# Values of two batches' contexts made in the router's tail and passed through device memory to the last attention of a two-layer decoder

## The chip, the cores and the metric

The kernel runs on one core of a Trainium2 chip. The metric is the device time of one execution in microseconds (us), the median of several runs. A run with a profile gives in addition a record of every instruction on the engines: PE (matmuls; PEld is its weight loads), DVE (vector), ACT (scalar), POOL (GpSimd), and SP, which here only issues DMA transfers. Each engine takes its instructions in one order that is fixed when the program is built, and waits on semaphores for what other engines and transfers have to finish.

## The reference

A decoder of two layers works on x (4 batches, 512 tokens, 256 features, float32) with a context of 1601 tokens of 256 features for each batch. After each step the sum with x is normalised. The steps are:

1. layer 0: a sequential fast-weight recurrence over the tokens;
2. layer 0: cross attention with one head on the context, with an additive mask;
3. layer 0: a mixture of 8 experts, of which a router picks 2 for each token;
4. layer 1: causal self attention with 16 heads of 16 features;
5. layer 1: cross attention on the same context with 16 heads and rotary positions;
6. layer 1: a feed-forward block with quantised weights.

The parts that the change touches, cut from the reference:

```python
# step 3, for each token
probs = softmax(xf @ Wr + br)
topw, topi = top_k(probs, 2)
# step 5
K = (key @ Wk.T + bk)        # key and value are the context, (4, 1601, 256)
V = (value @ Wv.T + bv)      # split into 16 heads of 16
out = softmax(rope(Q) @ rope(K).T / 4) @ V
x = layernorm(x + out @ Wo.T + bo)
```

The bias `bv` is folded into the bias after the output product, so the kernel's values are the plain product of the context with `Wv`. They depend on inputs alone and could be made at any time.

## The kernel before

Everything is float32. Tokens lie in tiles of 128 partitions: a batch's x is 4 such tiles (`x[b]`), its transpose is `xT[b]`, and a context is 13 key tiles, the last with 65 rows. The program is a sequence of stages. Within most of them the order of the instructions on every engine is the order of the Python program (`manual_schedule`), written out by hand; between them a scheduler may interleave.

**Step 2 and the router.** The loop over 16 steps (batch, token tile) computes scores with `ctxT`, exponents, transposed weights and the weighted context. When a batch is through, a generator `closing(b)` is put into the list `tails`; each call of `tail()` runs it to its next `yield`. It normalises the batch (`rstd_ln`: two ACT instructions), transposes it into `xT[b]` (eight PE transposes and one ACT copy, lines 188 and 196), and runs `route(b)`: four groups of products with `Wr` (8 columns wide), an exp on ACT (line 470), a chain of small DVE instructions that pick two experts, two products that count rows before (`before`, `full`), and DVE instructions that make `rows`. `scatter(b)` (line 534) then writes the batch's rows to their experts' places in `xs` in device memory, by eight indirect DMAs that POOL issues. The scatters of batches 0 to 2 are ordered among each other: each waits until the one before has landed. Those of batch 3 are declared free of order. For batches 0 to 2 the generator's pieces lie between other batches' steps. For batch 3 nothing is left to lie between: the last loop, `while tails: tail()`, runs it alone. PSUM tiles called `bank` come from a pool of two, tiles called `wide` from a pool of three.

**The experts.** `begin(i)` loads the 256 rows of block i (`xb`, line 835) and its weights `eWi` and `eWg`; `first_half` loads `eWo`. Blocks follow one another on PE with 48 matmuls of 256 columns each (two records in the trace for each matmul). Eight weights of layer 1 (`W`, 256 KB each) are loaded on SP before the first block; their tiles lie where the tiles of step 2 lay, and wait for those.

**Layer 1.** There are 32 units (batch, group of four heads, self or cross), first the 16 of the self attention, then the 16 of the cross attention, batch by batch. In a cross unit a loop runs over 13 key tiles. Each step computes four score tiles (line 1315), their exponents on ACT (line 1329), the weighted values of the tile before (`po`, line 1342), and two slots of the next unit's row maxima (PE line 202, `one<-kc,qt`, and DVE line 1272). Work of other kinds is spread over the steps from the list `extras[i]` of unit i, one item behind a step. Where a step has an item, `po` is computed 512 columns wide in one piece; where it has none, in two pieces of 256, each in one half of the step (`filled`).

Items of the list are, among others, the keys and values of later batches, made by `context(b, keys, values)`: a key item is two matmuls of 512 columns with a part of the context (`cx`, loaded by `chunk`), an ACT copy with bias and a rotation on POOL, after which the rows go through device memory (`kcd`); a value item is two matmuls of 256 columns with `W["xaV"]` and an ACT copy (line 1196) that puts 16 heads of 16 columns at a distance of 17 into `vals[b % 2]`. The free 17th column holds 1.0 and the last 15 columns 0.0, set once by `values_tile`. Values and keys of batches 0 and 1 are made earlier, around the start of layer 1. For batches 2 and 3 the list `later` deals them out: to the four cross units of batch 0 the keys of batch 2 and half of those of batch 3, to those of batch 1 the other half and the 13 value items of batch 2, to those of batch 2 the 13 value items of batch 3. Work that has to run at the start of a unit lies in `starts[i]`; the loads of `kc` are there.

Of the kernel before, what the change touches and what calls it, by code (L numbers as in the profile page):

```python
# [9 lines left out]
F32 = mybir.dt.float32  # L10
# [7 lines left out]
P = 128  # L18
B, S, D = 4, 512, 256
S2 = 1601  # L20
NT = S // P
NKT = (S2 + P - 1) // P
# [3 lines left out]
NH, HD = 16, 16  # L26
# [8 lines left out]
def kn_of(kt):  # L35
    return P if kt < NKT - 1 else KLAST
# [3 lines left out]
def decoder(ctx: ExitStack, tc: tile.TileContext, a: dict, out: bass.AP):  # L40
    nc = tc.nc
# [13 lines left out]
    def wide():  # L55
        return psum["A"].tile([P, 2, 512], F32, tag="wide", name="wide")

    def bank():
        return psum["B"].tile([P, 512], F32, tag="bank", name="bank")
# [15 lines left out]
    def weight(pool, name):  # L75

        src = a[name]
        t = pool.tile([P, 2, src.shape[1]], F32, tag=name, name=name)
        nc.sync.dma_start(t, src.rearrange("(c p) n -> p c n", p=P))
        return t  # L80
# [117 lines left out]
    def mm(ps, terms):  # L198

        n = len(terms)  # L200
        for i, (l, r) in enumerate(terms):
            nc.tensor.matmul(ps, l, r, start=(i == 0), stop=(i == n - 1))  # L202
# [3 lines left out]
    p2in = ph2in.enter_context(tc.tile_pool(name="p2in", bufs=1))  # L206


    with (
# [15 lines left out]
        ps = wide()  # L225
# [4 lines left out]
        ps = bank()  # L230
# [7 lines left out]
        fs = p2in.tile([P, NT, S2], F32, tag="fs", name="fs")  # L238
# [7 lines left out]
        KHALF = (NKT + 1) // 2  # L246
# [281 lines left out]
    def scatter(b, done=lambda inst: None):  # L528

        rows = placed[b]  # L530
        for t in range(NT):
            for k in range(2):
                done(
                    nc.gpsimd.indirect_dma_start(
                        xs, bass.IndirectOffsetOnAxis(ap=rows[:, k * NT + t : k * NT + t + 1], axis=0), x[b][:, t, :], None
                    )
                )
# [67 lines left out]
        return wrow, xrow  # L605


    with tc.tile_pool(name="p2", bufs=2) as p2, ExitStack() as ordered:


# [5 lines left out]
        ps = wide()  # L616
# [3 lines left out]
        ps = bank()  # L620
# [3 lines left out]
        ps = wide()  # L624
# [3 lines left out]
        ps = bank()  # L628
# [25 lines left out]
        def scored(b, t):  # L654

            blk = slice(t * P, (t + 1) * P)
            sc = p2.tile([P, S2], F32, tag="sc", name="sc")
            mx = small.tile([P, 2], F32, tag="mx", name="mx")
            for h, (k0, kw) in enumerate(parts):
                ps = wide()  # L660
                flat = ps.rearrange("p a n -> p (a n)")
                for s0 in range(0, kw, 512):
                    s1 = min(s0 + 512, kw)
                    mm(
                        flat[:, s0:s1],
                        [(qs[b][:, c, blk], ctxTs[b][:, c, k0 + s0 : k0 + s1]) for c in range(2)],
                    )
                nc.vector.tensor_tensor_reduce(
                    out=sc[:, k0 : k0 + kw],
                    in0=flat[:, :kw],  # L670
                    in1=fs[:, t, k0 : k0 + kw],
                    scale=1.0,
                    scalar=LOWEST,
                    op0=ALU.add,
                    op1=ALU.max,
                    accum_out=mx[:, h : h + 1],
                )
            nm = small.tile([P, 1], F32, tag="nm", name="nm")
            nc.vector.tensor_reduce(nm, mx, AX.X, ALU.max, negate=True)
            sm = small.tile([P, 1], F32, tag="sm", name="sm")  # L680
            nc.scalar.activation(sc, sc, AF.Exp, bias=nm, accum_out=sm)
            scs[b, t], sums[b, t] = sc, sm
# [59 lines left out]
        scored(*steps[0])  # L742
        tails = []

        def tail():
            if tails and next(tails[0], tails) is tails:
                tails.pop(0)

        for i in range(len(steps) + 1):
            if i + 1 < len(steps):  # L750
                b, t = steps[i + 1]
                scored(b, t)
                if t == NT - 1:
                    more_columns(b + 2)
                    if b + 1 < B:
                        queries(b + 1)
            tail()
            if i < len(steps):
                turned(*steps[i])
            tail()  # L760
            if i > 0:
                b, t = steps[i - 1]
                weighted(b, t)
                if t == NT - 1:
                    if b + 1 < B:
                        ctxns[b + 1] = load_ctx(b + 1)
                    tails.append(closing(b))
            tail()
        while tails:
            tail()  # L770
        ordered.close()
        scatter(B - 1, lambda inst: unordered("xs", inst))
        wrow, xrow = blocks_left()
# [5 lines left out]


    QS = 1.0 / math.sqrt(HD)
    VW = HD + 1
    p4a = late_a.enter_context(tc.tile_pool(name="p4a", bufs=1))
    mrow = tc.dram_tile((4 * B, S2), F32, name="mrow")
    live = p4a.tile([P, 4 * B], F32, tag="live", name="live")
# [27 lines left out]
    def values_tile(pool, name, n):  # L813
        t = pool.tile([P, n, NH * VW + HD - 1], F32, tag=name, name=name)
        nc.gpsimd.memset(t[:, :, NH * VW :], 0.0)
        heads = t[:, :, : NH * VW].rearrange("p k (h r) -> p k h r", r=VW)
        nc.gpsimd.memset(heads[:, :, :, HD : HD + 1], 1.0)
# [210 lines left out]
    with ExitStack() as s4:  # L1028
# [149 lines left out]
        def context(b, keys, values, here=None):  # L1178


            def key(src, i, c, eng):
                flush(1)
                k0, kw = chunks[i]
                ps = one()
                mm(ps[:, :kw], [(W["xaK"][:, h, c * P : (c + 1) * P], src()[h][:, :kw]) for h in range(2)])
                raw = raw_tile()
                nc.scalar.activation(raw[:, :kw], ps[:, :kw], AF.Identity, bias=bkc[:, c : c + 1])
                rotated(raw, kw, slice(k0, k0 + kw), eng, ready["turn", i] if here else None)
                going.append(lambda: to_rows(kcd[b], c, k0, kw, raw[:, :kw]))

            def value(src, k):
                kn, c0 = kn_of(k), (k % 4) * P
                ps = one()[:, :D]
                mm(ps[:kn], [(src()[c][:, c0 : c0 + kn], W["xaV"][:, c, :]) for c in range(2)])
                dst = vals[b % 2][:kn, k, : NH * VW].rearrange("p (h r) -> p h r", r=VW)
                nc.scalar.copy(dst[:, :, :HD], ps[:kn].rearrange("p (h r) -> p h r", r=HD))

            items = []
            for i in sorted({*keys, *values}):
                if here is None:  # L1200
                    src = lambda n=len(stream): chunk(n)
                    stream.append((b, i))
                else:
                    src = lambda i=i: here[2 * i : 2 * i + 2]
                eng = nc.gpsimd if here is None else nc.vector
                if i in keys:
                    items += [lambda s=src, i=i, c=c: key(s, i, c, eng) for c in range(2)]
                if i in values:
                    items += [lambda s=src, k=k: value(s, k) for k in range(4 * i, min(4 * i + 4, NKT))]
            return items  # L1210
# [121 lines left out]
        def weighted(u, k, q0=0, q1=S):  # L1332
# [6 lines left out]
            for j in range(4):  # L1339
                ex = state["ex", u, k, j // 2]  # L1340
                c0 = (4 * g + j) * VW
                nc.tensor.matmul(  # L1342
# [227 lines left out]
        for b in range(1, B):  # L1570
            i = index[b - 1, 0, False]
# [11 lines left out]
        for b in range(B):  # L1583
            i = index[b - 1, 0, True] if b else index[B - 1, 0, False]
# [30 lines left out]
        flush(0)  # L1615
        for i, (n0, n1) in enumerate(((0, 4), (4, 6), (6, 7), (7, 8))):
            extras[i] = keys1[n0:n1] + extras[i]
        later = [
            context(2, range(4), ()) + context(3, range(2), ()),
            context(3, range(2, 4), ()) + context(2, (), range(4)),  # L1620
            context(3, (), range(4)),
        ]
        for b, work in enumerate(later):
            for g in range(NG):
                n = -(-len(work) // (NG - g))
# [5 lines left out]
        for b in range(B - 1):  # L1631
            i = index[b, NG - 1, True] + 2
# [10 lines left out]
        for i, u in enumerate(units):  # L1643
# [16 lines left out]
            for k in range(nk):  # L1660
# [13 lines left out]
                for half in range(2 if u != units[-1] else 0):  # L1674
                    first = scores(u, k, half, 0)
# [33 lines left out]
        rest = ending()  # L1709
# [149 lines left out]
```

## Time and profile before

| | |
|---|---|
| median of 3 runs | 2454.46 us (2454.04 to 2455.28) |
| the profiled execution | 2460.01 us, its span 2458.2 us |
| mean granted PE clock | 0.964 |
| busy: PE, DVE, ACT, POOL | 2349.0, 1187.0, 1074.2, 425.0 us |
| last products of step 2 to the first expert's transposes | 485.4 to 521.4 us |
| experts | 521.4 to about 1020 us |
| cross attention of layer 1 | about 1510 to 2334 us |

The page's second part divides the span into 40 equal slices of 61.5 us and gives the busy share of an engine in each as one digit, 9 for 90% or more. The timeline gives the start and the length in us, the engine, the line, the operation, `out<-in` by the names of the tiles, shapes, and how many instructions were merged (`x8`); in brackets stands how long the engine had been idle before and what ended that. `SPq` and `POOL ... DMA_INDIRECT` are the issues of transfers, not their landing. A stage table gives the busy time of each engine in a stretch, then the granted clock (1.00 is full), the DMA share and GB/s. A PE instruction's own length overlaps the next one's, so a chain is read from start to start.

### The profile page before, as it was taken

What the parts mean: (1) busy time and instruction counts of PE and PEld (TensorE: products, weight loads), DVE (VectorE), ACT (ScalarE), POOL (GpSimd) and SP (SyncE); (2) the same over time, 40 slices, a digit from 0 to 9 for tenths busy, and PEclk for the clock granted to TensorE, in tenths of its full rate; (3) what the DMA queues carried; (4) which work ended last, traced back from release to release, by engine and by line L of the source; (5) the groups of instructions that cost most, each with busy time, mean ns of one, the idle gap of its engine ahead of it and who ended that gap; (6) DMA issues with size and microseconds to landing.
All of it is one profiled execution on the core that took longest, in us unless ns stands there. A gap on an engine that the chain in (4) does not pass through costs nothing.

```text
span 2458.2 us, 34942 instructions
## 1 busy us (share of the span) xinstructions
PE 2349.0 (96%) x13928; PEld 1331.3 (54%) x13928; DVE 1187.0 (48%) x2772; ACT 1074.2 (44%) x1996; POOL 425.0 (17%) x431
## 2 busy tenths in 40 slices
PE   7998999959999999969999999999999999999998
PEld 4767677748888888743333334333333333333256
DVE  1333334422222222336666667666666666677334
ACT  1111222114455544324555553655566565556730
POOL 1010001121134444323330000222110010000000
PEclk9999999969999999978999998999999999999999
DMA  8300211234767555442211220122210110110100
GB/s 319 135 1 23 102 54 44 73 135 149 263 251 273 212 190 197 145 122 81 83 44 30 71 75 5 49 73 62 66 54 20 44 40 16 32 36 16 33 9 26
DMA packets 82513, 224.50 MB, mean 91 GB/s; under 512 B 14120, under 2 KB 37934, under 8 KB 73262
## 3 DMA queue, kind: packets, MB, share of 16 engines
q1 hardware_dynamic: 68190, 141.70, 17.1%
q0 software_dynamic: 10992, 65.54, 7.3%
q10 hardware_dynamic: 3168, 15.03, 1.8%
q8 instruction: 110, 1.80, 0.3%
q14 instruction: 53, 0.43, 0.1%
HBM read 171.53 MB, written 53.21 MB: 91 GB/s over the span
## 4 chain that ended last, share of the span: by engine, by line
PE 51%; ACT 1%; DVE 1%; issue 0%; DVEq 0%; ACTq 0%
PE s L1315 23%; PE one L202 12%; PE po L1342 11%; PE s L202 2%; PE s L1325 1%; PE one L1300 1%; PE one L1363 1%; ACT x L171 0%; ACT ex L1329 0%; DVE one L1274 0%; PE one L1384 0%; PE one L1405 0%; PE one L1482 0%; DVE pm L1272 0%; DVE st L156 0%
## 5 line engine op out<-in xcount | busy, mean ns | idle before, releaser
L1329 ACT ACTIVATE ex<-s 128x512 f32<-128x512 f32 (+1 forms) x1062 | 578.1, 594 | 480.5 <-PE s L1315 237.4
L1272 DVE TENSOR_REDUCE pm<-one 128x1 f32<-128x512 f32 x768 | 494.2, 686 | 203.7 <-PE s L1315 147.7
L1315 PE MATMUL s<-q,kc 32*128 32x512 f32 x1612 | 522.9, 640 | 0.2 <-ACT ex L1329 0.2
L202 PE MATMUL one<-kc,qt 32*128 32x512 f32 (+1 forms) x2048 | 483.6, 563 | 0.3 <-DVE pm L1272 0.3
L1315 PEld LDWEIGHTS s<-q,kc 32*128 32x128 f32 x1612 | 161.6, 179 | 210.2 <-issue 175.2
L1342 PE MATMUL po<-ex,v 128*32 128x256 f32 (+3 forms) x2472 | 245.8, 466 | 0.3 <-ACT ot L1355 0.3
L1274 DVE CUSTOM_DVE_ANT_0 one<-one,c_diagq 128x512 f32<-128x512 f32 x256 | 172.0, 716 | 89.2 <-PE one L202 78.3
L1315 PE MATMUL s<-q,ks 32*128 32x512 f32 x512 | 182.2, 660 | 4.9 <-ACT ex L1329 4.9
L1342 PEld LDWEIGHTS po<-ex,v 128*32 128x32 f32 (+1 forms) x2472 | 49.9, 108 | 233.0 <-issue 227.0
L886 DVE TENSOR_TENSOR g<-g,sg 128x1024 f32<-128x1024 f32 x46 | 57.3, 1246 | 238.3 <-ACT sg L883 238.3
L202 PE MATMUL wide<-xbT,eWi 128*128 128x256 f32 x736 | 168.4, 388 | 4.0 <-DVE xbT L858 4.0
L202 PEld LDWEIGHTS one<-kc,qt 32*128 32x128 f32 x2048 | 163.9, 188 | 11.7 <-DVE pm L1272 7.7
L202 PE MATMUL bank<-eWo,g 128*128 128x256 f32 x736 | 162.8, 379 | 0.5 <-DVE rb L899 0.5
L202 PE MATMUL wide<-xbT,eWg 128*128 128x256 f32 x736 | 162.9, 379 | 0.1
L202 PEld LDWEIGHTS wide<-xbT,eWi 128*128 128x128 f32 x736 | 143.6, 195 | 25.1 <-issue 3.4
L1155 POOL TENSOR_TENSOR raw<-raw,c_cos 128x512 f32<-128x512 f32 (+1 forms) x32 | 35.0, 1093 | 696.2 <-DMA swp<-raw 616.5
L202 PE MATMUL one<-ks,qt 32*128 32x512 f32 x512 | 153.4, 668 | 1.1 <-ACT raw L1126 1.1
L202 PEld LDWEIGHTS wide<-xbT,eWg 128*128 128x128 f32 x736 | 139.8, 190 | 19.5 <-ACT g L883 0.5
L202 PEld LDWEIGHTS bank<-eWo,g 128*128 128x128 f32 x736 | 138.1, 190 | 18.5 <-DVE rb L899 0.6
L883 ACT ACTIVATE g<-wide,eWi 128x256 f32<-128x256 f32 x184 | 71.9, 477 | 69.8 <-PE wide L202 67.0
L1315 PEld LDWEIGHTS s<-q,ks 32*128 32x128 f32 x512 | 54.1, 188 | 83.1 <-issue 61.9
L202 PE MATMUL wide<-ctxT,q 128*128 128x512 f32 (+1 forms) x256 | 91.3, 510 | 0.8 <-DVE q L649 0.8
(310 smaller groups left out, 2969.7 us busy)
## 6 DMA issues: line engine op xcount, KB each, us to landing
xs<-zero SPq DMA_DIRECT2D x32, 512.0 KB
kc<-kcd SPq DMA_DIRECT2D x16, 800.5 KB
eWo<-in_eWo SPq DMA_DIRECT2D x8, 1408.0 KB
cx<-in_ctxT SPq DMA_DIRECT2D x18, 512.0 KB
eWi<-in_eWi SPq DMA_DIRECT2D x8, 1028.0 KB
eWg<-in_eWg SPq DMA_DIRECT2D x8, 1028.0 KB
swp<-raw SPq DMA_DIRECT2D x64, 128.0 KB
qt<-qd SPq DMA_DIRECT2D x32, 256.0 KB
```

What stands on the lines that cost most here:

```text
L202: nc.tensor.matmul(ps, l, r, start=(i == 0), stop=(i == n - 1))
L883: nc.scalar.activation(dst[:, k, :], pv[:, k, :], func, bias=bias)
L886: nc.vector.tensor_tensor(part, part, dst, ALU.mult)
L1155: eng.tensor_tensor(raw[:, :n], raw[:, :n], cos[:, :n], ALU.mult)
L1272: nc.vector.tensor_reduce(pm[:, t, j, c : c + 1], ps, AX.X, ALU.max)
L1274: nc.vector.tensor_tensor_reduce(out=ps, in0=ps, in1=diagq[:, 384 - t * P : 896 - t * P], scale=1.0, scalar=LOWEST, op0=ALU.add, op1=ALU.m ...
L1300: nc.tensor.transpose(pt[:, t * P : (t + 1) * P], ng.rearrange("p j r -> p (j r)"), ident)
L1315: nc.tensor.matmul(ps[:kn], kt[rows, k * P : k * P + kn], q2[rows, :], start=True, stop=cross)
L1325: nc.tensor.matmul(ps[:, k * P : (k + 1) * P], later_[:, :P], later_[:, P:], start=False, stop=True)
L1329: nc.scalar.activation(ex[:kn, h, :], ps[:kn], AF.Exp)
L1342: nc.tensor.matmul(state["po"][j * 32 : j * 32 + 32, q0:q1], (vals if cross else vself)[b % 2][:kn, k, c0 : c0 + 32], ex[:kn, j % 2, q0:q1 ...
L1363: nc.tensor.transpose(pt[:, t * P : (t + 1) * P], ot[:, t * P : (t + 1) * P], ident)
```

## The change

The 26 value items of batches 2 and 3 are taken out of `later`. They are made in the last loop of the router instead, two behind each call of `tail()` while batch 3's generator runs, and the rest after it. `xaV` gets a second copy in the pool `p2`, loaded at that stage's start. The results stand in two tiles that take the places of `fs` (the mask, last read by batch 3's scores) and `ctxa` (half of batch 3's context), laid out with the 17th columns and the 15 zero columns, which six POOL memsets write at the first value. Each batch's values then go to device memory (`vd`, 1.9 MB), batch 2's in two stores and batch 3's in one. The cross units (1,1) and (2,1) load them into `vals` at their start. The keys of batches 2 and 3 are now dealt out as eight items to the units of batch 0 and eight to those of batch 1.

```diff
+    VW = HD + 1
+    VROW = NH * VW + HD - 1
+    vd = {b: tc.dram_tile((P, NKT * VROW), F32, name=f"vd{b}") for b in (2, 3)}
...
+        xaV = weight(p2, "xaV")
+        values, places = [], {}
+
+        def value(b, k):
+            if not places:
+                big = p2in.tile([P, NT * S2], F32, tag="fs", name="v23")
+                rest = p2in.tile([P, KHALF * D], F32, tag="ctxa", name="v2")
...
+                for b_ in (2, 3):
+                    nc.gpsimd.memset(places[b_, NKT - 1], 0.0)
+                for t in (big[:, : 22 * VROW], rest[:, : 4 * VROW]):
+                    t = t.rearrange("p (k r) -> p k r", r=VROW)
+                    nc.gpsimd.memset(t[:, :, NH * VW :], 0.0)
+                    heads = t[:, :, : NH * VW].rearrange("p k (h r) -> p k h r", r=VW)
+                    nc.gpsimd.memset(heads[:, :, :, HD : HD + 1], 1.0)
+            kn = kn_of(k)
+            ps = bank()[:, :D]
+            mm(ps[:kn], [(ctxTs[b][:, c, k * P : k * P + kn], xaV[:, c, :]) for c in range(2)])
+            dst = places[b, k][:kn, : NH * VW].rearrange("p (h r) -> p h r", r=VW)
+            nc.scalar.copy(dst[:, :, :HD], ps[:kn].rearrange("p (h r) -> p h r", r=HD))
+            if b == 2 and k == NKT - 1:
+                nc.sync.dma_start(vd[2][:, : 9 * VROW], big_of(2, 0, 9))
+                nc.sync.dma_start(vd[2][:, 9 * VROW :], big_of(2, 9, NKT))
+            if b == 3 and k == NKT - 1:
+                nc.sync.dma_start(vd[3], big_of(3, 0, NKT))
...
+        values = [lambda b=b, k=k: value(b, k) for b in (2, 3) for k in range(NKT)]
         while tails:
             tail()
+            for f in values[:2]:
+                f()
+            values = values[2:]
+        for f in values:
+            f()
         ordered.close()
         scatter(B - 1, lambda inst: unordered("xs", inst))
...
-        later = [
-            context(2, range(4), ()) + context(3, range(2), ()),
-            context(3, range(2, 4), ()) + context(2, (), range(4)),
-            context(3, (), range(4)),
-        ]
+        later = [context(2, range(4), ()), context(3, range(4), ())]
+        for b in (2, 3):
+            starts[index[b - 1, 1, True]].append(
+                lambda b=b: nc.sync.dma_start(vals[b % 2].rearrange("p k r -> p (k r)"), vd[b])
+            )
```

More of the change, by code (lines that the diff above doesn't have):

```diff
@@ L743, in decoder, with big_of @@
         tails = []
+        xaV = weight(p2, "xaV")
[4 more added lines that the diff above has]
+                rest = p2in.tile([P, KHALF * D], F32, tag="ctxa", name="v2")
+                for i in range(NKT):
+                    places[3, i] = big[:, i * VROW : (i + 1) * VROW]
+                    j = NKT + i
+                    places[2, i] = (
+                        big[:, j * VROW : (j + 1) * VROW] if i < 9 else rest[:, (i - 9) * VROW : (i - 8) * VROW]
+                    )
[16 more added lines that the diff above has]
+                nc.sync.dma_start(vd[3], big_of(3, 0, NKT))
+        def big_of(b, k0, k1):
+            first = places[b, k0]
+            return bass.AP(first.tensor, first.offset, [first.ap[0], [1, (k1 - k0) * VROW]])
         def tail():
@@ L781, in decoder @@
     QS = 1.0 / math.sqrt(HD)
-    VW = HD + 1
     p4a = late_a.enter_context(tc.tile_pool(name="p4a", bufs=1))
@@ L1617, in decoder @@
             extras[i] = keys1[n0:n1] + extras[i]
-        later = [
-            context(2, range(4), ()) + context(3, range(2), ()),
-            context(3, range(2, 4), ()) + context(2, (), range(4)),
-            context(3, (), range(4)),
-        ]
+        later = [context(2, range(4), ()), context(3, range(4), ())]
+        for b in (2, 3):
+            starts[index[b - 1, 1, True]].append(
+                lambda b=b: nc.sync.dma_start(vals[b % 2].rearrange("p k r -> p (k r)"), vd[b])
+            )
         for b, work in enumerate(later):
```

## The prediction

> **What bounds the kernel now.** I read the page's slices first, then a table by stage, then the timeline of the two places the change touches.
>
> ```profile
> PE   7998999959999999969999999999999999999998
> 485.40:521.40 36.00, 9.96 (x39) 8.67 (x40) 13.86 (x76) 3.03 (x5) 13.48 (x14) 0.54 0.39 129
> 1510.00:2334.00 824.00, 823.49 (x6444) 286.83 (x6443) 534.39 (x964) 505.13 (x951) 90.23 (x74) 1.00 0.13 41
> ```
>
> The columns of the last two are busy PE, PEld, DVE, ACT, POOL, then clock, DMA share and GB/s. In the router's tail (485.4 to 521.4) PE works 10 of 36 us at clock 0.54; in the last attention it is full at clock 1.00. Work taken from the second place is time; work put into the first is free only where the tail's own chain doesn't queue behind it. That chain and its neighbour on POOL:
>
> ```profile
> 485.39 0.37 SPq L79 DMA_DIRECT2D qkvQ<-in_qkvQ  x1
> 486.68 0.96 POOL L534 DMA_INDIRECT xs<-x,rows  x1 [1.73 <-DMA xs<-x,rows]
> 487.83 0.20 ACT L127 ACTIVATE rstd<-sd 128x4 f32<-128x4 f32 x1
> 488.54 2.30 PE L188 MATMUL wide<-ident,x 128*128 128x128 f32 x8 [3.19 <-DVE x L726]
> 490.88 1.01 ACT L196 COPY xT<-wide 128x1024 f32<-128x1024 f32 x1 [2.84 <-PE wide L188]
> 491.94 1.02 PE L202 MATMUL bank<-Wr,xT 128*128 128x8 f32 x4 [1.10 <-ACT xT L196]
> 492.42 0.96 POOL L534 DMA_INDIRECT xs<-x,rows  x1 [4.78 <-DMA xs<-x,rows]
> ...
> 498.62 0.23 ACT L470 ACTIVATE lg<-lg 128x32 f32<-128x32 f32 x1 [6.73 <-DVE lg L469]
> 503.79 0.63 PE L202 MATMUL bank<-both,before 128*128 128x32 f32 x2 [5.88 <-DVE both L492]
> 504.83 0.96 POOL L534 DMA_INDIRECT xs<-x,rows  x1 [1.95 <-DMA xs<-x,rows]
> 507.09 0.96 POOL L534 DMA_INDIRECT xs<-x,rows  x1 [1.30 <-DVE cum L562]
> 518.52 0.89 SPq L835 DMA_DIRECT2D xb<-xs  x2
> 521.36 1.09 PE L854 MATMUL bank<-ident,xb 128*128 128x128 f32 x4 [15.87 <-DMA xb<-xs]
> ```
>
> Batch 3 goes rstd, x, transposes, xT copy, Wr products, exp, picks, ranks, rows, eight row scatters from 507.09, first expert at 521.36. Meanwhile POOL is still on batch 2's eight scatters (481.32 to 505.79): each waits until the one before has landed.
>
> The last attention, PE alone:
>
> ```profile
> 2016.63 1.06 PE L1342 MATMUL po<-ex,v 128*32 128x512 f32 x8
> 2018.70 1.13 PE L202 MATMUL one<-xaV,cx 128*128 128x256 f32 x4
> 2020.83 0.64 PE L1342 MATMUL po<-ex,v 128*32 128x256 f32 x8
> 2022.62 0.64 PE L1342 MATMUL po<-ex,v 128*32 128x256 f32 x8
> 2024.32 1.07 PE L1342 MATMUL po<-ex,v 128*32 128x512 f32 x8
> ```
>
> A step over one key tile with a value item runs from the 512-wide `po` at 2016.63 to 2020.83, 4.20 us; the next, with none, splits `po` in two and ends at 2024.32, 3.49 us.
>
> **Part 1, taken from the last attention: -18.5 us.** 26 value items leave (two matmuls and an ACT copy each). An item's own 1.06 us isn't the price, since the empty step splits `po` and waits a little; the difference of the steps is: 4.20 - 3.49 = 0.71. 26 x 0.71 = 18.5. Bounds from whole units (distance of their `ot` copies): unit (2,2) with three values 51.31 against (3,2) with none 48.75, 0.85 each, 22 us; (2,0) with four 55.34 against (3,0) 53.55, 0.45 each, 12 us. I take 0.71: it is the same in nearly every value step from 1800 to 2075. Four key items move from batch 0's units to batch 1's, same price in both. Eight `cx` loads go; nothing waited for them.
>
> **Part 2, the new loads: 0.** `vals` comes in one 1.9 MB load at the start of unit (1,1) and (2,1). The tile's last reader is one unit earlier, so SP isn't held; its reader starts three units (158 us) later. The first expert's `eWo` with three `xb` (2.2 MB) took 519.45 to 527.97, so 8 us is the size. Without that cover a load would cost its 8 us.
>
> **Part 3, added to the router's tail: +21.0 us.** In the built program's order, ACT has, after batch 3's `rstd`, four value copies before the xT copy, six before exp; the first waits for PE and for POOL. POOL's six memsets stand behind all eight scatters of batch 2. So ACT, and behind it the xT copy and all of batch 3, waits for POOL. On the axis of before:
> - POOL. Third scatter 486.68. The 5.74 and 4.16 us steps that follow fall in the 2 MB of W loads from 485.39, which now wait behind the value stores; the quiet step is 2.67. 486.68 + 5 x 2.67 + 0.96 = 501.0. (At the old pace 505.8, 4.8 more: bound.)
> - Memsets. From 128x1024 952 ns and 128x128 203 ns a plain one of 287 is 0.34; from 195 in 270 and 208 in 453 the strided ones of 330 and 352 are 0.39 and 0.70. Four of them with POOL's 0.3 step: 503.1.
> - Two copies of 0.37, then values 3 and 4 (two PSUM banks, so they wait for copies 1 and 2) at the half clock, 9.96/32 x 4 = 1.24 each: 506.0. Transposes 2.30, xT copy 1.01: 509.35 instead of 491.89, +17.5.
> - Values 5 to 8 stand before Wr on PE, 1.24 each and, once the clock is up, 0.92 (0.88 by the expert's 7.07/32 x 4, and a little for waits): 512.4 instead of 491.94, +20.5.
> - Wr takes 5.97 (491.94 to 497.91) at clock 0.50; batch 2's, at 1.00, took 3.4 (459.41 to 462.80). The values keep PE busy from 503.5, and the expert at 523.23 got its clock after 5.7 us of that, so I take 3.4: ends 515.8, +17.9.
> - Values 9 and 10 and their copies before exp: 2 x 0.92 + 0.45, exp at 518.1, +19.5.
> - Values 11 to 18, 8 x 0.92 = 7.4 from 517.7, end at 525.1; DVE has `both` at 503.73 + 19.5 = 523.2. PE is late: `before` product +21.3.
> - The DVE steps to `rows` no longer interleave with the block count: 1.3 instead of 1.7. Scatter of batch 3 +21.0, first expert the same.
>
> Values 19 to 26 (7.4 us) end near 533, before the expert at 542: hidden. Eight W loads, moved behind the stores, are first read after 1000 us: hidden.
>
> [...]
>
> ```profile
> 490.00:495.00 5.00, 3.90 (x17) 3.40 (x16) 0.00 (x0) 1.01 (x1) 0.96 (x1) 0.50 0.87 281
> 528.00:529.00 1.00, 1.00 (x4) 0.74 (x3) 0.00 (x0) 0.00 (x0) 1.00 (x1) 0.54 0.02 5
> 529.00:530.00 1.00, 1.00 (x6) 0.88 (x5) 0.00 (x0) 0.22 (x1) 0.23 (x1) 1.00 0.00 0
> ```
>
> PE 78% busy with 8-wide products stays at 0.50; wide matmuls raise it at 529. [...]
>
> By the rows the clock may sink in Wr. If it never rises, values 5 to 8 end at 513.3, Wr at 519.3, exp starts at 522.2, values 11 to 18 end at 531.7: the scatters come at +27.5.
>
> **Sum.** +21.0 - 18.5 = +2.5 us. The profiled execution took 2460.0 (span 2458.2), 5.5 above the median of the runs; it goes to 2462.5, the median from 2454.5 to 2457.0. Ends: router +19 (clock up from value 3 on) to +27.5 (or +25.8 at the old scatter pace), attention -12 to -22.
>
> **Rivals.**
> - *Slower: the clock stays at 0.50, or the scatters keep their old pace.* Place: the tail. For it: 0.50 from 488 to 528 in before, though PE was busy at 490. Against: wide work now fills 503 to 533. Price +27.5 - 18.5 = +9.0, 2463.5; with old scatters +25.8 - 18.5 = +7.3, 2461.8. It decides once the tail costs over 23.4.
> - *Slower: the stores delay the experts.* The second store stands on SP between `xb` of experts 0 and 1; the W loads wait for it, and expert 2's weights stand behind them, due 567.75 + 21 = 588.8. From 539.5 that is 8.1 MB in 49 us, 165 GB/s; 276 to 350 GB/s ran at 520 to 526. At 300 the last byte is there at 566.5, 22 us early; at 150 it is 5 late: 2462. It decides below 165.
> - *Faster: ACT isn't held.* If the copies ran at 488, the values would cost the chain only PE time: values 3, 4, 7, 8, 10 and the 1.9 us at `both`, less Wr's gain of 2.6, about +5. Then 5 - 18.5 = -13.5: 2441. Against: POOL's order. It needs POOL free before 493.
> - *Faster by the attention alone*, 22 saved, router +19: -3, inside no change.
>
> **How the numbers follow.** 0.2% (4.9 us) is about what a measurement here tells from no change. Forecast with its bounds, -3 to +4.9: 0.52. Clock or scatters: 0.25. Stores: 0.10, with other new waits of the tail 0.13. ACT not held, or a larger gain: 0.10. So faster 0.10, same 0.52, slower 0.38. The range 2450 to 2465 leaves out about 0.1 at each end: below, ACT not held; above, both slow causes together or late weights. The likeliest case alone is 2451.5 to 2459.4.
>
> **What would show it.** Right: in the profile after, ACT idle some 15 us before the first `v23` copy, ended by POOL's memset; scatters of batch 2 at an even 2.67; xT copy near 508, exp near 518, batch 3's scatters from about 528, first expert's transposes near 542; last attention 805 instead of 824, empty steps of 3.49 where values were. Wrong: the first copy before 495 (2441); clock 0.50 until after Wr (2463.5); PE waiting for `eWi` or `xb` of experts 1 to 3; steps of the last attention not shorter, by DVE or ACT taking over, which would leave all 21.

## The result, and the profile after

The changed kernel took 2456.38 us (median; 2450.80 to 2458.69) against 2455.39 us (2453.42 to 2462.55) of the kernel before on the same chip: ratio 0.9996 with a 95% interval of 0.9985 to 1.0007. Nothing that can be measured was gained or lost. The profiled execution took 2451.01 us, its span is 2449.2 us.

Page of the kernel after: the span, and the busy tenths of PE in 40 slices.

```profile
span 2449.2 us, 35374 instructions
...
PE   7998999879999999979999999999999999999998
```

The ninth slice (490 to 551 us), a 5 before, is now a 7; the router's tail lies in it. To read the two places alike in every kernel I cut them at fixed marks: the *tail* from batch 3's `rstd` to the first expert's transposes, the *attention* from the copy of the last self-attention's `ot` to that of the last cross unit's. Tables by stage, columns as in the prediction; first the kernel before:

```profile
487.83:521.36 33.53, 9.92 (x38) 8.63 (x39) 11.79 (x67) 2.73 (x4) 12.51 (x13) 0.50 0.38 124
1508.86:2334.38 825.52, 825.00 (x6453) 287.33 (x6454) 534.48 (x964) 505.79 (x953) 90.23 (x74) 1.00 0.13 41
```

and the same stretches of the kernel after:

```profile
484.87:538.36 53.49, 31.05 (x134) 26.42 (x135) 11.37 (x60) 12.13 (x30) 14.20 (x19) 0.76 0.21 82
1519.28:2325.24 805.96, 805.20 (x6565) 278.70 (x6565) 533.78 (x964) 497.49 (x926) 90.21 (x74) 1.00 0.13 42
```

The tail is 19.96 us longer, the attention 19.56 us shorter. Both places moved by 20 us, and they cancel.

The chain of the tail, timeline of the kernel after (POOL's scatters and memsets, ACT and PE):

```profile
484.87 0.20 ACT L127 ACTIVATE rstd<-sd 128x4 f32<-128x4 f32 x1
...
495.36 0.96 POOL L534 DMA_INDIRECT xs<-x,rows  x1 [1.71 <-DMA xs<-x,rows]
496.32 0.62 POOL L765 MEMSET v<- 128x287 f32 x2
497.00 0.39 POOL L768 MEMSET v<- 128x330 f32 x1
497.45 0.69 POOL L770 MEMSET v<- 128x352 f32 x1
...
498.17 0.65 ACT L775 COPY v<-bank 128x256 f32<-128x256 f32 x2 [13.10 <-POOL v L770]
...
502.17 1.04 PE L188 MATMUL wide<-ident,x 128*128 128x128 f32 x8
...
503.25 1.01 ACT L196 COPY xT<-wide 128x1024 f32<-128x1024 f32 x1 [0.50 <-PE wide L188]
...
506.51 0.51 PE L202 MATMUL bank<-Wr,xT 128*128 128x8 f32 x4
...
510.45 11.54 PE L202 MATMUL bank<-xaV,ctxT 128*128 128x256 f32 x40
...
512.56 0.37 ACT L775 COPY v<-bank 128x256 f32<-128x256 f32 x1 [5.48 <-PE bank L202]
514.27 0.37 ACT L775 COPY v<-bank 128x256 f32<-128x256 f32 x1 [1.33 <-PE bank L202]
514.53 0.23 ACT L470 ACTIVATE lg<-lg 128x32 f32<-128x32 f32 x1
...
521.83 0.30 PE L202 MATMUL bank<-both,before 128*128 128x32 f32 x2
...
524.01 0.97 POOL L534 DMA_INDIRECT xs<-x,rows  x1 [25.71 <-DVE rows L521]
...
538.36 1.09 PE L900 MATMUL bank<-ident,xb 128*128 128x128 f32 x4 [8.62 <-DMA xb<-xs]
```

ACT stands idle for 13.10 us in front of the first value copy, released by POOL's memset, which stands behind eight scatters. Behind that copy stands the xT copy, and behind it the whole of batch 3's routing: xT, `Wr` (506.51), exp (514.53), ranks (521.83), scatters (524.01), first expert (538.36). Batch 2's last scatters are issued at an even 2.67 us (492.69 the one before that shown).

The attention, timeline of PE in the kernel after, around the place shown in the prediction:

```profile
2013.73 0.64 PE L1388 MATMUL po<-ex,v 128*32 128x256 f32 x8
...
2017.22 0.64 PE L1388 MATMUL po<-ex,v 128*32 128x256 f32 x8
```

Between these two lies one step, 3.49 us: what an empty step cost before, with no value item in it.

### The profile page after: what moved, and what is told of

It is laid out like the page before. It is cut to its first block, busy times and chain, and to the rows that moved or that the text cites. A ratio compares the mean times of both kernels' runs of the same rounds, so it can differ in the third digit from the quotient of the medians.

```text
span 2449.2 us, 35374 instructions
## 1 busy us (share of the span) xinstructions
PE 2342.8 (96%) x14144; PEld 1336.1 (55%) x14144; DVE 1187.7 (48%) x2772; ACT 1075.4 (44%) x1996; POOL 428.8 (18%) x437
## 4 chain that ended last, share of the span: by engine, by line
PE 50%; ACT 1%; DVE 1%; issue 0%; DVEq 0%; ACTq 0%
PE s L1361 23%; PE po L1388 12%; PE one L202 11%; PE s L202 2%; PE s L1371 1%; PE one L1346 1%; PE one L1409 1%; ACT x L171 0%; ACT ex L1375 0%; DVE one L1320 0%; PE one L1430 0%; PE one L1528 0%; PE one L1451 0%; DVE pm L1318 0%; DVE st L156 0%
## 5 line engine op out<-in xcount | busy, mean ns | idle before, releaser
L1388 PE MATMUL po<-ex,v 128*32 128x256 f32 (+3 forms) x2688 | 250.9, 442 | 0.3 <-ACT ot L1401 0.3
L202 PEld LDWEIGHTS wide<-xbT,eWi 128*128 128x128 f32 x736 | 141.9, 193 | 24.4 <-issue 3.4
L202 PEld LDWEIGHTS bank<-eWo,g 128*128 128x128 f32 x736 | 138.1, 190 | 18.5 <-DVE rb L945 0.6
```

The costliest lines, as they stand in the source:

```text
L1388: nc.tensor.matmul(state["po"][j * 32 : j * 32 + 32, q0:q1], (vals if cross else vself)[b % 2][:kn, k, c0 : c0 + 32], ex[:kn, j % 2, q0:q1 ...
```

## The experiments

My theory: the tail's +20 is made up of a wait for POOL's memsets (some 16 us) and the values' own work on PE (some 4), the attention's gain is 0.7 us for each value, and keys, loads and stores cost nothing. The rivals are that the values' work itself makes the tail longer, that the re-dealt keys make part of the attention's change, and that the stores matter. Each run was compared with the kernel before on the same chip. Of each profile I read the two stretches; the table collects them.

| run | tail, us | attention, us | both against before | median against before | ratio [95%] |
|---|---|---|---|---|---|
| before | 33.53 | 825.52 | | | |
| after | 53.49 | 805.96 | +0.4 | +1.0 | 0.9996 [0.9985, 1.0007] |
| e1_memsets_first | 37.03 | 805.87 | -16.2 | -16.4 | 0.9931 [0.9909, 0.9952] |
| e3_wait_without_work | 45.24 | 804.77 | -9.0 | -9.7 | 0.9959 [0.9944, 0.9974] |
| e2_attention_alone | 35.44 | 805.06 | -18.6 | -21.8 | 0.9913 [0.9887, 0.9940] |
| e6_keys_only | 33.50 | 823.57 | -2.0 | -1.8 | 0.9993 [0.9982, 1.0004] |
| e4_half | 30.12 | 820.05 | -8.9 | -15.3 | 0.9936 [0.9916, 0.9956] |
| e7_double_stores | 53.53 | 807.53 | +2.0 | -0.5 | 1.0001 [0.9988, 1.0013] |
| e5_spread | 32.80 | 805.87 | -20.4 | -19.6 | 0.9916 [0.9889, 0.9943] |
| e8_count_first | 33.30 | 810.33 | -15.4 | -16.5 | 0.9939 [0.9918, 0.9959] |
| e9_no_early_stores | 33.58 | 806.08 | -19.4 | -17.1 | 0.9935 [0.9920, 0.9949] |
| e10_no_early_stores_spread | 33.15 | 805.96 | -19.9 | -24.4 | 0.9910 [0.9891, 0.9928] |

The two stretches of the one profiled execution explain the difference of the medians to within 3.2 us in all but e4 and e10 (6.4 and 4.5); how much chance moves the rest of the program is told in the last section.

### e1_memsets_first: the wait taken away

The memsets of the large tile are issued ahead of batch 2's scatters; `constant` writes the zero columns and the 17th columns of a tile, as in the changed kernel.

```diff
+        def early():
+            big = p2in.tile([P, NT * S2], F32, tag="fs", name="v23")
+            ...
+            nc.gpsimd.memset(places[3, NKT - 1], 0.0)
+            constant(big[:, : 22 * VROW])
...
                 scored(b, t)
+                if i + 1 == len(steps) - 1:
+                    early()
```

> The constants of the large tile are written by POOL ahead of batch 2's eight scatters, as soon as the mask's last reader is through; all else as in the changed kernel. Theory (the tail's 20 us are mostly ACT held for POOL): the first value copy comes right behind batch 3's rstd, the 13 us of idle ACT are gone, and what is left in the chain is PE work of values 3, 4, 7 to 10 and a late count product, 4 to 5 us; attention still 19.6 shorter: 2455.4 - 19.6 + 4.5 = 2440 (2437 to 2444). Rival (the PE work of the values, at a low clock, is the price and the wait only hides it): still within 3 us of the changed kernel, 2453 to 2459.

Measured: 2438.35 us, ratio 0.9931 [0.9909, 0.9952]. Timeline of ACT and PE in this run:

```profile
484.52 0.20 ACT L127 ACTIVATE rstd<-sd 128x4 f32<-128x4 f32 x1
484.63 0.63 ACT L778 COPY v<-bank 128x256 f32<-128x256 f32 x2
...
487.95 1.01 ACT L196 COPY xT<-wide 128x1024 f32<-128x1024 f32 x1 [0.50 <-PE wide L188]
...
498.18 0.23 ACT L470 ACTIVATE lg<-lg 128x32 f32<-128x32 f32 x1
...
521.55 1.09 PE L905 MATMUL bank<-ident,xb 128*128 128x128 f32 x4 [8.69 <-DMA xb<-xs]
```

The first copies follow `rstd` by 0.1 us instead of 13.3, and the tail falls from 53.49 to 37.03. With the same values on the same engines, taking the wait away saves 16.5 of the 20 us; 3.5 is what the values' work costs the chain without it.

### e3_wait_without_work: the wait kept, the work taken away

Only the first value is computed; DVE fills the two tiles with ones in place of the rest.

```diff
+                nc.vector.memset(big[:, : 22 * VROW], 1.0)
+                nc.vector.memset(rest[:, : 4 * VROW], 1.0)
...
-            kn = kn_of(k)
-            ps = bank()[:, :D]
-            mm(ps[:kn], ...)
-            nc.scalar.copy(dst[:, :, :HD], ...)
+            if b == 2 and k == 0:
+                kn = kn_of(k)
+                ...
+                nc.scalar.copy(dst[:, :, :HD], ...)
```

> Of the 26 values only the first is computed, its copy behind POOL's memsets as in the changed kernel; the other 25 are left out (tiles filled with ones by DVE before). Theory: ACT is held until POOL's memset near 498, the transposes of batch 3 no longer wait for values, so the xT copy comes at about 498.6 instead of 487.9, 10.6 late, and nothing else is late: 2436 + 10.6 = 2446.5 (2444 to 2450). Rival (the work is the price): as without any values, 2436.

Measured: 2445.05 us, ratio 0.9959 [0.9944, 0.9974]. Timeline of ACT in this run:

```profile
490.86 0.20 ACT L127 ACTIVATE rstd<-sd 128x4 f32<-128x4 f32 x1
505.82 0.37 ACT L778 COPY v<-bank 128x256 f32<-128x256 f32 x1 [14.76 <-POOL v L772]
506.09 1.02 ACT L196 COPY xT<-wide 128x1024 f32<-128x1024 f32 x1
```

One copy of 0.37 us that has to wait is enough: the xT copy comes 15.2 us behind `rstd` (before: 3.05), and the tail is 11.7 us longer with 25 of 26 values gone. The work itself isn't needed for most of the loss. Some 1.7 of the 11.7 us belong to this profile and not to the edit: batch 2's scatters begin 6.5 us before `rstd` here and 8.2 us before it in the changed kernel, so the wait counted from `rstd` is longer (the account of the prediction below says what goes along with that); with the changed kernel's lead it would be some 10 us, an estimate from the two leads. The two parts don't simply add: 10 to 11.7 by the wait alone, 3.5 by the work alone, 20.0 together. Together the values also have to be made after the wait, in the chain's own time: four before xT, four before `Wr`, two before exp, part of them at half clock (granted 0.50 up to 502.1 and from 509.0 to 515.8 in the kernel after).

### e2_attention_alone: neither wait nor work

```diff
-                for b_ in (2, 3):
-                    nc.gpsimd.memset(places[b_, NKT - 1], 0.0)
-                ...
-            mm(ps[:kn], ...)
-            nc.scalar.copy(dst[:, :, :HD], ...)
+                nc.vector.memset(big[:, : 22 * VROW], 1.0)
+                nc.vector.memset(rest[:, : 4 * VROW], 1.0)
```

> The 26 value products and copies are left out altogether (the two tiles are filled with ones by DVE); the stores, the loads and the attention are those of the changed kernel. Theory: the tail is as before, no ACT wait, the attention is 19.6 shorter, and the stores and loads cost nothing: 2455.4 - 19.6 = 2436 (2433 to 2439). Rival (stores delay the experts or the attention's gain was luck of one profile): 2442 or more.

Measured: 2432.97 us, ratio 0.9913 [0.9887, 0.9940], a hair below the expected range: the attention's whole gain shows up when no values are made in the tail. The tail is still 1.9 us longer, where it was expected as before. Timeline of SP and POOL in this run:

```profile
492.52 0.34 SPq L767 DMA_DIRECT2D vd<-v  x1
493.73 0.34 SPq L768 DMA_DIRECT2D vd<-v  x1
494.11 1.26 SPq L770 DMA_DIRECT2D vd<-v  x1
497.67 0.96 POOL L534 DMA_INDIRECT xs<-x,rows  x1 [4.59 <-DMA xs<-x,rows]
505.54 0.98 POOL L534 DMA_INDIRECT xs<-x,rows  x1 [6.92 <-DVE yf L595]
```

With nothing to compute, all three stores (3.8 MB) are issued between 492.52 and 494.11, while a scatter is under way, and the wait before the next scatter is 4.59 us instead of 1.71. Batch 3's first scatter follows 21.2 us behind `rstd` (before: 19.3), though its `rows` are ready 18.9 us behind `rstd`, as early as before (19.0). The profile puts its wait down to a DVE instruction (`yf`) that doesn't feed `rows`; what held it isn't shown.

### e6_keys_only and e4_half: the attention's two parts

Only the keys dealt out as in the changed kernel, values left where they were:

```diff
-            context(2, range(4), ()) + context(3, range(2), ()),
-            context(3, range(2, 4), ()) + context(2, (), range(4)),
+            context(2, range(4), ()),
+            context(3, range(4), ()) + context(2, (), range(4)),
             context(3, (), range(4)),
```

> The kernel before with only the keys dealt out anew (eight items to batch 0's units, eight to batch 1's together with batch 2's 13 values, batch 3's values to batch 2's). Theory: a key item has the same price everywhere, cross attention 825.5 +- 1, time as before, 2455 +- 3. Rival (the new places of the keys bring part of the 19.6): cross attention 2 us or more shorter.

Measured: 2454.77 us, ratio 0.9993 [0.9982, 1.0004]. The time is as expected; the attention is 823.57 us, 1.95 shorter and so outside the 1 us that the expectation allowed, close to the rival's 2 us.

Only batch 3's 13 values moved, in the manner of e5:

```diff
-    vd = {b: tc.dram_tile((P, NKT * VROW), F32, name=f"vd{b}") for b in (2, 3)}
+    vd = {b: tc.dram_tile((P, NKT * VROW), F32, name=f"vd{b}") for b in (3,)}
...
-        later = [context(2, range(4), ()), context(3, range(4), ())]
+        later = [context(2, range(4), ()), context(3, range(4), ()) + context(2, (), range(4))]
```

> Only batch 3's 13 values are made in the router's tail, early constants and spread as in the run before; batch 2's stay items of the attention units of batch 1. Theory (a price per value step, 19.6/26 = 0.75 us): the cross attention takes 825.5 - 9.8 = 815.7 us and the tail the 33 us of before: 2455 - 10 = 2445 (2441 to 2449). Rival (the gain comes from the keys' new places or from the loads that went): closer to 806 than to 816.

Measured: 2441.26 us, ratio 0.9936 [0.9916, 0.9956], in the expected range, but the profile's attention was 820.05 instead of 815.7, and its tail 30.12 instead of 33.

The distances of the units' `ot` copies, summed by batch, sort this out (us):

| units of batch | before | e6 | e4 | after |
|---|---|---|---|---|
| 0 | 217.79 | 210.90 | 211.94 | 211.15 |
| 1 | 215.12 | 221.60 | 223.26 | 213.53 |
| 2 | 213.05 | 213.13 | 203.73 | 203.35 |
| 3 | 179.56 | 177.94 | 181.12 | 177.93 |

Moving four keys takes 6.9 us from batch 0's units and puts 6.5 on batch 1's: nothing net, as predicted. Thirteen values are worth 9.4 us in batch 2's units (e6 to e4: 0.72 each) and 8.1 in batch 1's (e6 to after: 0.62 each). Batch 3's units were never touched, and yet they are 1.6 us longer in the kernel before, 3.2 in e4. Table by stage of the kernel before, at that place:

```profile
2208.37:2211.78 3.41, 3.41 (x16) 0.58 (x16) 1.46 (x6) 1.67 (x3) 0.00 (x0) 0.51 0.02 5
```

For 3.41 us PE ran at a clock of 0.51, busy all the time; that costs 1.7 us, an estimate (3.41 x 0.49). In e4 the clock is 0.50 for 2.1 us at the attention's start and for 6.8 us near 2200, by the same estimate some 4.5 us lost, which is what its profile has over the 815.7; e8 has the same two places (810.33), e5 none (805.87). In batch 3's units, after and e6 have none either. So of the 19.56 us between the two profiles 1.6 are such a stretch, and the change's own share is 18.0. The same 1.6 explain most of the 1.95 in e6, where the keys alone leave 0.4.

### e7_double_stores: the stores twice

Each store is issued a second time, into another place in device memory (`vx`).

```diff
+                nc.sync.dma_start(vx[:, : 9 * VROW], big_of(2, 0, 9))
+                nc.sync.dma_start(vx[:, 9 * VROW :], big_of(2, 9, NKT))
...
+                nc.sync.dma_start(vx, big_of(3, 0, NKT))
```

> The changed kernel with each store of values made a second time, to another place in device memory: 3.8 MB more on SP's queue, before the rows and the weights of the first experts. Theory (stores are hidden): tail 53.5 us from rstd to the first expert, no wait of PE for rows or weights of experts 1 to 3, 2456 (2453 to 2460). Rival (stores delay the experts): 5 us or more longer than the changed kernel, with PE waiting for a load after the first expert.

Measured: 2456.06 us, ratio 1.0001 [0.9988, 1.0013]. What PE waited for over all experts in the kernel after (engine, line, what it waited for; total, number, longest):

```profile
PE bank L900 <- DMA xb<-xs: 8.6, 1, 8.6
PE wide L202 <- DVE xbT L904: 4.0, 2, 3.2
PE bank L202 <- DVE rb L945: 0.5, 1, 0.5
PE wide L202 <- ACT g L929: 0.3, 1, 0.3
```

Only the first expert's `xb` is waited for, no weights and no later `xb`. With twice the stores the first three waits read 8.5, 4.0 and 0.5 and the fourth isn't there. In their place in the changed kernel the stores cost nothing that can be measured.

### e5_spread: the values where PE waits

On top of e1, the values are no longer made two by two but where the chain leaves PE idle: 8 of them before the ranks, 18 behind them.

```diff
+        counts = [2, 0, 1, 0, 0, 2, 2, 1]
         while tails:
             tail()
-            for f in values[:2]:
+            n = counts.pop(0) if counts else 0
+            for f in values[:n]:
                 f()
-            values = values[2:]
+            values = values[n:]
```

> The constants as early as in the first of these runs, and the values dealt out by where PE idles: two while batch 3 is normalised, one during the xT copy, five during the picks, eighteen during batch 3's scatters. Theory: no value lies on the chain, PE stays warm for the Wr products (3.4 instead of 6.0) and for the first expert (up to 2.9 less): 2455.4 - 19.6 - 3 = 2433 (2429 to 2437). Rival (the work is the price): 2440 to 2456.

Measured: 2435.15 us, ratio 0.9916 [0.9889, 0.9943]; like e1 it beats both kernels. Table by stage of its tail:

```profile
484.88:517.68 32.80, 28.53 (x135) 23.89 (x135) 10.77 (x56) 12.11 (x30) 12.95 (x16) 0.95 0.36 134
```

The tail is now 0.7 us shorter than before the change, with 26 values in it. PE works 28.5 of 32.8 us, and its clock is 0.95 where it was 0.50. One wait was left that looked removable. Timeline of PE in this run:

```profile
514.47 0.28 PE L202 MATMUL bank<-carry,full 128*128 128x8 f32 x2
517.68 0.63 PE L907 MATMUL bank<-ident,xb 128*128 128x128 f32 x4 [2.93 <-DVE wf L579]
```

### e8, e9, e10: what ends the tail now, two wrong guesses

The block count (`wf`) starts with the carry product, and that stands behind the last 18 values. e8 moves it ahead of them:

```diff
             values = values[n:]
+        wrow, xrow = blocks_left()
         for f in values:
             f()
         ordered.close()
         scatter(B - 1, lambda inst: unordered("xs", inst))
-        wrow, xrow = blocks_left()
```

> The spread version once more (its memsets before batch 2's scatters, its values in the gaps), with one thing moved: the products that count the blocks left (the carry, wrow and xrow) are issued ahead of the last 18 values instead of behind them, so that VectorE's count of blocks can end before the first expert's transposes. In the spread version these transposes waited 2.93 us for VectorE's wf. If that wait is what ends last there, the stretch from rstd to the first expert's transposes falls from 32.8 to about 30 us (29.9 to 30.9: the landing of xb comes next) and the median from 2435 to about 2432.5 us (2427 to 2437). Rival: the last 18 values (about 6.7 us of TensorE between the last token block's work and the expert) are on the path themselves, as TensorE's own queue; then the wait becomes TensorE's work, the stretch stays at 32 to 33 us and the median at 2435.

Measured: 2438.56 us, ratio 0.9939 [0.9918, 0.9959], tail 33.30: no gain. The wait for `wf` is gone, and in its place stands one for `xb`, just as long. Timeline of PE in this run:

```profile
505.13 16.14 PE L202 MATMUL bank<-xaV,ctxT 128*128 128x256 f32 x72
524.11 0.63 PE L907 MATMUL bank<-ident,xb 128*128 128x128 f32 x4 [2.84 <-DMA xb<-xs]
```

SP issued the load of `xb` 5.83 us after the last scatter (515.47 to 521.30), in e5 5.03; in before, after, e1 and e2 the same distance is 2.5. In e5 and e8 a store of batch 2 was issued 5.7 and 4.9 us before that scatter, and after e2 I suspected the stores. e9 and e10 leave batch 2's stores out of e8 and e5; batch 2's units then read batch 3's values:

```diff
-            if b == 2 and k == NKT - 1:
-                nc.sync.dma_start(vd[2][:, : 9 * VROW], big_of(2, 0, 9))
-                nc.sync.dma_start(vd[2][:, 9 * VROW :], big_of(2, 9, NKT))
```

> As the version with the block count first, but batch 2's two stores are left out (1.9 MB), and batch 2's units read batch 3's values in their place, so that the output is not the reference's; all 26 values are still computed and batch 3's store stays where it was. Suspected cause: with a store of batch 2 issued 4.9 to 5.7 us before the last of batch 3's scatters, the load of xb followed that scatter's issue by 5.0 and 5.8 us; in the four traces with no store so near it followed by 2.5. If the stores are the cause, xb is issued 2.5 to 2.6 us after the last scatter and the first expert's transposes stand 30 to 30.8 us behind rstd instead of 33.3, the median 2 to 3 us below the block-count version's 2438.6 (2433 to 2439 with its scatter). Rival: the delay comes from somewhere else (the values on TensorE and ScalarE, the scatters' own order); then the distance stays at 5 or more and the stretch at 33.

> The same stores left out of the spread version (batch 2's units read batch 3's values, the output is not the reference's), whose block count stays behind the last values. If the stores hold xb and the block count is the next wait, xb is issued 2.5 us after the last scatter here too, but the first expert's transposes now wait for VectorE's wf alone: about 32.5 us behind rstd (32 to 33), no gain over the spread version, median 2435 (2430 to 2440). Rival: the count is not on the path; then 30 to 30.8 us here as well.

Measured: e9 2435.58 us, ratio 0.9935 [0.9920, 0.9949], tail 33.58, distance 5.88; e10 2428.32 us, ratio 0.9910 [0.9891, 0.9928], tail 33.15, distance 5.08. The stores aren't it. e10's lower median doesn't come from the tail; its profile has the shortest middle of the program of all (last section), and whether more than chance is in that stays open. The waits of SP's own queue in e8 say more:

```profile
SPq L888 <- DMA xs<-x,rows: 7.0, 1, 7.0
...
SPq L888 <- PE bank L202: 3.4, 1, 3.4
```

After the scatter has landed, the load of `xb` waits 3.4 us more for a product on PE (e5: 2.7): the last value's, which ends at 521.27, and SP issues at 521.30. In `after` and e1 the values end before the last scatter lands, so this wait is already over there. The last values are on the path after all, as the rival of e8 said, though not through PE's queue but through SP. In e5, e9 and e10 it is the same: the last value's product ends at 514.63, 514.93 and 514.37, and SP issues `xb` within 0.1 us of it (514.66, 515.01, 514.45). e4 shows the other side: with 5 values behind the ranks instead of 18, PE is through at 508.29 and stands idle for 11.72 us until `xb` has landed (520.01; in e5 it is idle for 2.93), and the tail is 30.12 us, the shortest of all. So the 18 values behind the ranks are what the last 2.5 to 3 us of e5 hang on. What ties `xb`'s load to the last product (the place it is put in is my guess) isn't shown.

## Why the prediction was right

Forecast 2457.0 us (2450 to 2465), no measurable change; measured 2456.38. Both terms held: tail +21.0 forecast, +19.96 measured; attention -18.5 forecast, -18.0 measured without the half-clock stretch, -19.56 with it.

The tail, step by step, each time counted from batch 3's `rstd`:

| step | forecast | after |
|---|---|---|
| POOL through with batch 2's scatters | +13.2 | +11.45 |
| first value copy (behind four memsets) | +15.3 | +13.30 |
| transposes start | +18.2 | +17.30 |
| xT copy ends | +21.5 | +19.39 |
| `Wr` starts | +24.6 | +21.64 |
| `Wr` ends | +28.0 | +25.58 |
| exp | +30.3 | +29.66 |
| `before` product | +37.3 | +36.96 |
| batch 3's first scatter | +40.3 | +39.14 |
| first expert | +54.5 | +53.49 |

- **The wait for POOL** was right in kind and 2.0 us too long in size. The pace of 2.67 held; but batch 2's scatters began 8.2 us before `rstd` in this profile, 6.5 in that of before. That lead isn't the change's doing. In this profile PE was granted 0.50 for one stretch of 3.41 us that ended 6.6 us before `rstd` (474.87 to 478.28); in before the clock is 1.00 from 467.6 to 487.9. The 14 products with `ctxa` at that place take 4.95 us here and in e5 (lead 8.2), 3.27 in before, e3 and e8 (lead 6.5). ACT's wait before batch 3's `sd` and `rstd` differs by as much: 16.66 us in the changed kernel, e1, e4, e5, e6, e7, e9 and e10, 14.97 or 14.98 in before, e3 and e8. With the lead of before, the wait would have ended at about +13.1 (forecast +13.2), and the tail would have been some +21.7: an estimate from the two leads. The memsets' prices held (0.31, 0.39 and 0.69 measured; 0.34, 0.39 and 0.70 forecast).
- **Values at half clock** were underestimated: 1.24 us each forecast, 1.7 measured (copies at 512.56 and 514.27). The step that failed is the division 9.96/32: that row of before runs from 523.23 and the clock comes up at 529, so it mixes both clocks. The transposes and the xT copy were overestimated by 1.2 for the opposite reason: the clock came up just then (0.50 up to 502.1, a mean of 0.98 from 502.00 to 506.50).
- **The clock** came up with the values, as forecast, and then did what the prediction had named as possible but left out of its sum: it sank in `Wr`. Table by stage of the kernel after, the clock third from the end:

```profile
502.00:506.50 4.50, 4.50 (x25) 3.92 (x24) 0.00 (x0) 2.41 (x5) 0.00 (x0) 0.98 0.00 0
506.51:510.45 3.94, 3.94 (x26) 3.76 (x24) 0.00 (x0) 0.37 (x1) 0.00 (x0) 0.82 0.00 0
510.45:512.00 1.55, 1.55 (x5) 1.28 (x5) 0.57 (x3) 0.00 (x0) 0.00 (x0) 0.50 0.00 0
512.00:514.50 2.50, 2.50 (x8) 1.96 (x7) 0.00 (x0) 0.61 (x2) 0.00 (x0) 0.50 0.32 131
```

 `Wr` cost 3.94 us (forecast 3.4), and values 9 and 10 with their copies 4.1 between `Wr` and exp (forecast 2.3). At the start of `Wr` the chain was 3.0 us ahead of the forecast, at exp 0.6: 2.3 us given back. The forecast met its size partly by errors of opposite sign, and partly by the lead of this profile; that is luck.
- **The attention.** 0.71 for each value, read from two neighbouring steps, against 0.72 (batch 2's units) and 0.62 (batch 1's) measured. The unit distances that gave the bounds (0.45 and 0.85) bracket it. Re-dealt keys net to -0.4 (e6).
- **Loads, stores, weights at nothing**: right (e7, and the waits of PE).
- **The rivals.** The clock at 0.50 until after `Wr`: not so, it was 0.98 from 502. Scatters at their old pace: an even 2.67. Stores that delay the experts: none waited. "ACT isn't held" didn't happen in the changed kernel, but e1 made its condition true and then landed where that rival had put it: 2438 against 2441, the values' own price +3.5 against about +5.

## What to carry to other kernels

When work is moved into an idle stretch, look at what else its first instruction brings along: 1.8 us of memsets (496.32 to 498.1) on a queue with eight scatters ahead of it cost 16 us (e1; 10 to 12 with nearly all values gone, e3), because a copy on ACT waited for them with the critical chain behind it (in e3 the transposes were through at 493.3, and the xT copy came at 506.09, behind the value copy of 505.82). Put set-up of a buffer on its queue before that queue's long waits, and hand the moved work out where the chain waits; then the same 26 items were free (tail 32.80 against 33.53), since PE's clock was also up with them: 0.95 over e5's tail against 0.50 in before and in e2, which makes no values there; the `Wr` products took 3.44 us in e5 (clock 0.99) and 5.97 before (0.50). When a wait is named, ask what else comes within the same microseconds: removing `wf`'s wait uncovered one of the same length, and the queue's own waits named it.

## What the runs showed of the hardware

- **A busy PE was granted half clock.** In before from 2208.27 for 3.41 us (table above), with PE busy throughout. In the changed kernel the clock fell during the 3.94 us of 8-wide `Wr` products, which follow one another without a gap: their mean of 0.82 puts the fall some 2.5 us into them, and it was still 0.50 at 514.50, 4 us after wide products had begun again. In e5 the same `Wr` ran at 0.99 and the stretch right behind it (492.07 to 498.00) at 0.72, with PE busy for all 5.93 us. So stretches that the profile shows as busy ran at half clock and at full: busy time as the profile shows it doesn't decide alone. What else does isn't shown.
- **The middle of the program differs from run to run by more than this change.** From the first expert to the last self-attention the twelve profiles took between 974.0 and 987.5 us; the seven whose PE instructions were counted there (before, after, e1, e2, e3, e5, e10) all have 4936. Tables by stage, first of before, then of e10:

```profile
521.36:1508.86 987.50, 950.83 (x4936) 627.19 (x4940) 421.60 (x1067) 446.99 (x871) 275.33 (x275) 0.95 0.41 141
```

```profile
517.46:1491.44 973.98, 937.45 (x4936) 623.90 (x4940) 424.08 (x1080) 446.76 (x871) 274.57 (x275) 0.97 0.42 147
```

 In these seven the granted clock goes along with it: 0.95 where the middle took 980.9 us or more, 0.96 at 977.6, 0.97 at 974.8 and 974.0. The changed kernel's profile is 9 us shorter than before's for this reason (980.92 here, and 484.87 against 487.83 up to `rstd`), while the medians agree; single spans can't be compared; stages can, apart from half-clock stretches like those above.
- **The wait before an indirect scatter was longer next to plain transfers.** The wait before the next scatter was 4.59 us next to e2's 3.8 MB of stores and 4.78 next to the weight loads that start at 485.39 in the kernel before, against 1.71 at the even pace. The coincidence in time is all that shows it; in e5 and e8 a wait of 2.39 and 2.60 us came up without a store near.
